# One projection bank between the quarters of row numbers, later weight loads behind the first gather, 38 warming transposes

## The chip, the cores and the metric

The kernel runs on one core of one Trainium2 chip. A core has five engines that run side by side, each with its own ordered instruction queue: TensorE (PE in the profile, with its weight loads listed as PEld), VectorE (DVE), ScalarE (ACT), GpSimd (POOL) and SyncE (SP), which here only issues transfers. Sixteen DMA engines move data between HBM and the on-chip memory. The metric is the device time of one execution in microseconds; the time before is the median of 3 runs.

## The reference

The input is `x`, 4096 tokens of 256 numbers, in float32. With `xn = layernorm(x)` the output is `x + attn(xn) + ffn(xn)`:

```python
# attn: local attention, 8 heads of 32, windows of 64 tokens, each query sees keys within 64
q, k, v = xn @ Wq + bq, xn @ Wk + bk, xn @ Wv + bv
p = softmax(where(abs(i - j) <= 64, q @ k.T * 32**-0.5, -1e30))
y = layernorm(xn + (p @ v) @ Wo + bo) * gamma + beta
attn = y + gelu(y @ W1 + b1) @ W2 + b2               # 256 -> 1024 -> 256
# ffn: mixture of 8 experts, the best 2 for each token
s = softmax(xn @ gate_w.T + gate_b);  top_w, top_idx = top_k(s, 2);  top_w /= top_w.sum()
ffn = sum over the 2 chosen e of top_w * (silu((xn @ gp_w[e].T + gp_b[e]) * (xn @ up_w[e].T + up_b[e]))
                                          @ down_w[e].T + down_b[e])   # 256 -> 816 -> 256
```

## The kernel before

All engines run in an order written out by hand (`manual_schedule`): each engine executes its instructions in the order in which the program issues them, and waits only on semaphores for its operands or for a buffer to come free.

**First part (lines 348 to 801).** Eight groups of 512 tokens are loaded (`load`), normalised (`stats`, `normal`: one group's rows are split over VectorE, ScalarE and POOL in group 0, later mostly POOL), stored to the DRAM table `xnd`, and transposed on TensorE (`turn`, L473). While the first load is in flight TensorE runs `WARM` transposes of the identity (L547), which write a bank that nobody reads. Router logits are taken from the transposed tokens (`logits`). Between these steps TensorE works off a list of 26 projection banks (`work`, handed out by `deal`): queries, keys and values of the first groups, each 512 columns wide, evacuated by ScalarE.

Then VectorE finds each token's two experts and, by prefix sums over counts, the place (`slot`) of each token in a table sorted by expert. The inverse table, which token stands in each row of the sorted table, is computed on TensorE. For each of four quarters of the 2 x 4096 slots VectorE builds two one-hot arrays, `in_row` (L753) and `in_col` (L758, then multiplied by the token number, L762), in two buffers each, and TensorE adds 16 products of them into the PSUM bank `found` (L764). After each of the first three quarters one projection bank is dealt (L771 and L772); the remaining three of the list are issued behind the last quarter (L782). `token` (L780) is `found` as integers.

Between the quarters VectorE also computes, in the pieces of `experts()`, which expert each unit uses (`expert`, L745). At the end of that piece SP loads unit 0's gate and up weights, unit 0's down weights and unit 1's gate and up weights (L746). The address of such a load is a value that SP reads from the `expert` table in on-chip memory (`value_load`, L207 and L215).

**Middle part (from line 1240).** The sorted table is worked off in units of 256 rows (or 128). For each, POOL gathers the unit's rows from `xnd` by indirect DMA, one per 128 rows (`gather`, L819), TensorE transposes them (`turned`, L832), ScalarE copies the first unit's transposes from PSUM (L837), and `chunk` runs the six 128-wide slices of the gated layer (L845), `down` the second product (L896, L907). Before the loop two gathers are issued (L1240), the remainder rows of `hT` are cleared (L1244), and the first residual tile is loaded on SP's queue and gets `bo` added on POOL (`residual`, L1066 and L1067).

Each of the first 32 steps of the loop also does one attention step for two tiles of 128 queries and four heads: scores on TensorE (L960), masked with their row minimum taken on VectorE (L974), exponentials on ScalarE (L989), the halves of each window merged on POOL (`merge`, L1001 and L1002), scaling on VectorE (`scale`, L1021), transposition on TensorE (`flip`, L1030). In step 0 TensorE's order is: scores, unit 0's transposes, chunks 0 and 1, unit 1's transposes, chunks 2 and 3, the flip, chunk 4. POOL's order in step 0 is: the residual's addition, unit 2's gather, the two subtractions of `apart` (L1009), then the merges. SP's order is: the three weight loads of L746, the residual, unit 1's down weights.

The last part runs the units that exist only for some routings (`whole`) and the second layer of the attention block (`hidden`, `second`); nothing in it is touched.

Of the kernel before, what the change touches and what calls it, by code (L numbers as in the profile page):

```python
# [34 lines left out]
I32 = mybir.dt.int32  # L35
# [6 lines left out]
P = 128  # L42
# [44 lines left out]
BLOCKS = len(UNITS)  # L87
# [4 lines left out]
DN = FCE * D + D  # L92
HQ = 4
AHEAD = 4
WARM = 50
EPS = 1e-5
MASKED = -1e30
LOWEST = -3e38
# [3 lines left out]
def block_kernel(ctx: ExitStack, tc: tile.TileContext, a: dict, out: bass.AP):  # L102
    nc = tc.nc
# [4 lines left out]
    def pool(stack, name, side=left, bufs=1, **kw):  # L108
        return stack.enter_context(
            tc.tile_pool(name=name, bufs=bufs, side=side, reuse_waits="tile", **kw)  # L110
        )

    const = pool(ctx, "const")
# [13 lines left out]
    def bank(name):  # L127
        return psm.tile([P, G], F32, tag="bank", name=name)
# [28 lines left out]
    slot = const.tile([P, 2, NT], I32, tag="slot", name="slot")  # L157
    share = const.tile([P, 2, NT], F32, tag="share", name="share")
    expert = const.tile([P, BLOCKS], I32, tag="expert", name="expert")
    token = const.tile([P, TILES], I32, tag="token", name="token")  # L160
    used = const.tile([P, len(MAYBE)], I32, tag="used", name="used")
    mv2 = const.tile([P, NT, 2], F32, tag="mv2", name="mv2")

    def bcast(ap, n, at):

        shape = list(ap.shape)
        shape.insert(at, n)
        return ap.unsqueeze(at).to_broadcast(shape)
# [29 lines left out]

    def expert_of(b):
        column = UNITS[b][2]  # L200
        return expert[0:1, column : column + 1]


    other = {}

    def load_gu(b):
        e = nc.sync.value_load(expert_of(b), min_val=0, max_val=E - 1)  # L207
        w = other.get(b, wexp).tile([P, GU], F32, tag="wg", name=f"wg{b}")
        nc.sync.dma_start(
            out=w, in_=a["gate_up"][bass.ds(e, 1), :, :].rearrange("e p n -> p (e n)")  # L210
        )
        return w

    def load_down(b):
        e = nc.sync.value_load(expert_of(b), min_val=0, max_val=E - 1)  # L215
        w = other.get(b, wexp).tile([P, DN], F32, tag="wd", name=f"wd{b}")
        nc.sync.dma_start(out=w, in_=a["down"][bass.ds(e, 1), :, :].rearrange("e p n -> p (e n)"))
        return w
# [129 lines left out]
    with ExitStack() as early:  # L348
# [64 lines left out]
        with ExitStack() as ln:  # L413
            xin = pool(ln, "xin", bufs=4)
            mvs, xs, xns, roots, scales = {}, {}, {}, {}, {}
# [112 lines left out]
            def deal(n):  # L528
                for _ in range(n):
                    list(next(todo))  # L530
# [14 lines left out]
            idle = bank("idle")  # L545
            for n in range(WARM):
                nc.tensor.transpose(idle[:, n % TG * P : (n % TG + 1) * P], ident, ident)  # L547
            copies = []
            for g in range(NG + 3):
# [37 lines left out]
                if 2 < g <= NG + 1 or g == 1:  # L587
                    n = max(g - 2, 0)
# [125 lines left out]
        def ended(name, numbers, n, ends_at):  # L714
            t = route.tile([P, n, E - 1], F32, tag=name, name=name)
            nc.vector.tensor_tensor(
                t, bcast(numbers, E - 1, 2), bcast(ends_at, n, 1), ALU.is_ge
            )
            return t

        def experts():

            expert_f = route.tile([P, BLOCKS], F32, tag="expert_f", name="expert_f")
            of_odd = route.tile([P, SINGLES], F32, tag="of_odd", name="of_odd")
            paired = route.tile([P, SINGLES], F32, tag="paired", name="paired")
            pe = ended("pair_e", pair_no[:, 0:BLOCKS], BLOCKS, pairs_to[:, 0 : E - 1])
            oe = ended("odd_e", single_no, SINGLES, odds[:, 1:E])
            nc.vector.tensor_tensor(
                paired,
                pair_no[:, PAIRS:BLOCKS],  # L730
                pairs_to[:, E - 1 :].to_broadcast([P, SINGLES]),
                ALU.is_lt,
            )
            yield
            single_e = expert_f[:, PAIRS:]
            nc.vector.tensor_reduce(expert_f, pe, AX.X, ALU.add)
            nc.vector.tensor_reduce(of_odd, oe, AX.X, ALU.add)
            yield
            nc.vector.tensor_tensor(single_e, single_e, of_odd, ALU.subtract)
            yield  # L740
            nc.vector.tensor_tensor(single_e, single_e, paired, ALU.mult)
            yield
            nc.vector.tensor_tensor(single_e, single_e, of_odd, ALU.add)
            yield
            nc.vector.tensor_copy(expert, expert_f)  # L745
            gus[0], downs[0], gus[1] = load_gu(0), load_down(0), load_gu(1)  # L746

        gus, downs = {}, {}
        table = experts()
        for n in range(4):  # L750
            k, q = n // 2, slice(n % 2 * QT, (n % 2 + 1) * QT)
            in_row = onehot.tile([P, P, QT], F16, tag="in_row", name=f"in_row{n}")
            nc.vector.tensor_tensor(  # L753
                in_row, row_of, bcast(part_f[:, 0, k, q], P, 1), ALU.is_equal
            )
            next(table, None)
            in_col = onehot.tile([P, TILES, QT], F16, tag="in_col", name=f"in_col{n}")
            nc.vector.tensor_tensor(  # L758
                in_col, col_of, bcast(part_f[:, 1, k, q], TILES, 1), ALU.is_equal
            )  # L760
            next(table, None)
            nc.vector.tensor_tensor(in_col, in_col, bcast(number[:, q], TILES, 1), ALU.mult)  # L762
            for i in range(QT):
                nc.tensor.matmul(  # L764
                    found[:, 0:TILES],
                    in_row[:, :, i],
                    in_col[:, :, i],
                    start=(n == 0 and i == 0),
                    stop=(n == 3 and i == QT - 1),
                )  # L770
            if n < 3:  # L771
                deal(1)  # L772

        z = col("z")
# [32 lines left out]
    def own(b, tag, shape, **kw):  # L807

        where = he
        if b >= ALWAYS:  # L810
            where, tag, kw = late, f"{tag}{b}", {}
        return where.tile(shape, F32, tag=tag, name=f"{tag}_{b}", **kw)

    def gather(b):
        x = own(b, "xs", [P, UNITS[b][1] if b >= ALWAYS else TB, D], bufs=3)
        at, n, _ = UNITS[b]
        for t in range(n):
            i = at + t
            nc.gpsimd.indirect_dma_start(  # L819
                out=x[:, t, :],  # L820
                out_offset=None,
                in_=xnd,
                in_offset=bass.IndirectOffsetOnAxis(ap=token[:, i : i + 1], axis=0),
            )
        return x
# [411 lines left out]
    def store(g, t, n, acc):  # L1237
        nc.sync.dma_start(out=rows(out, g * TG + t, n), in_=acc[:, t : t + n, :])

    xs = {b: gather(b) for b in range(2)}  # L1240

    hTs = [he.tile([P, FCE, B], F32, tag=f"hT{k}", name=f"hT{k}", bufs=1) for k in range(2)]
    for k in range(2):
# [15 lines left out]
    for b in range(ALWAYS):  # L1259
# [103 lines left out]
        n = b - (ALWAYS - len(MAYBE))  # L1363
# [22 lines left out]
    for b in range(ALWAYS, BLOCKS):  # L1386
        at, n, _ = UNITS[b]
# [139 lines left out]
```

## Time and profile before

| what | us |
|---|---|
| median of 3 runs (1086.47 to 1089.2) | 1088.48 |
| the profiled execution, its own time | 1084.23 |
| its span, first to last instruction | 1082.1 |
| PE busy | 1068.8 (99%) |
| PEld busy | 857.1 (79%) |
| DVE busy | 657.5 (61%) |
| ACT busy | 526.7 (49%) |
| POOL busy | 451.6 (42%) |
| PE busy in the first 40 us, in 40 to 80, in 80 to 120 | 37.79, 39.59, 36.51 |
| DMA share in the same stretches | 0.75, 0.34, 0.35 |

A timeline line of the profile gives the start in us from the span's beginning, the busy time in us, the engine, the line of the kernel with operation, result and operands, how many instructions are merged, and in brackets how long the engine was idle before and what ended that idle time. A line of waits gives the engine and the waiting work, what it waited for, and then the sum in us, the number of times and the longest. A busy PE is not PE at its peak: matmuls are pipelined, and their ends are modelled.

### The profile page before, as it was taken

What the parts mean: (1) busy time and instruction counts of PE and PEld (TensorE: products, weight loads), DVE (VectorE), ACT (ScalarE), POOL (GpSimd) and SP (SyncE); (2) the same over time, 40 slices, a digit from 0 to 9 for tenths busy, and PEclk for the clock granted to TensorE, in tenths of its full rate; (3) what the DMA queues carried; (4) which work ended last, traced back from release to release, by engine and by line L of the source; (5) the groups of instructions that cost most, each with busy time, mean ns of one, the idle gap of its engine ahead of it and who ended that gap; (6) DMA issues with size and microseconds to landing.
All of it is one profiled execution on the core that took longest, in us unless ns stands there. A gap on an engine that the chain in (4) does not pass through costs nothing. (4 is left out here: it accounts for less than half of the span.)

```text
span 1082.1 us, 19049 instructions
## 1 busy us (share of the span) xinstructions
PE 1068.8 (99%) x6802; PEld 857.1 (79%) x6802; DVE 657.5 (61%) x1709; ACT 526.7 (49%) x1225; POOL 451.6 (42%) x599
## 2 busy tenths in 40 slices
PE   9998999999999999999999999999999999999998
PEld 6577887887888788888888888888788847777778
DVE  6665766657666566666666766666533355555546
ACT  4526456654556546746564566455424363333320
POOL 5516544455445444554455535544520043322220
PEclk9999999999999999999999999999999999999999
DMA  8252445544445354545444545445666443333121
GB/s 282 76 215 97 142 140 179 178 144 154 159 143 192 125 174 149 201 142 175 159 175 142 197 142 189 142 161 169 191 213 228 158 146 105 101 98 97 59 64 40
DMA packets 61040, 163.42 MB, mean 151 GB/s; under 512 B 6576, under 2 KB 46896, under 8 KB 51472
## 3 DMA queue, kind: packets, MB, share of 16 engines
q1 hardware_dynamic: 53632, 144.18, 38.2%
q0 software_dynamic: 6480, 17.70, 6.1%
q8 instruction: 55, 0.90, 0.3%
q10 hardware_dynamic: 832, 0.30, 0.1%
q14 instruction: 41, 0.34, 0.1%
HBM read 140.28 MB, written 21.89 MB: 150 GB/s over the span
## 5 line engine op out<-in xcount | busy, mean ns | idle before, releaser
L845 PE MATMUL gu<-xsT,wg 128*128 128x256 f32 (+1 forms) x1632 | 363.1, 369 | 1.6 <-issue 1.5
L845 PEld LDWEIGHTS gu<-xsT,wg 128*128 128x128 f32 x1632 | 289.0, 190 | 46.9 <-DVE nm L974 8.6
L853 ACT ACTIVATE gs<-gu,wg 128x256 f32<-128x256 f32 (+1 forms) x204 | 92.4, 453 | 257.8 <-PE gu L845 254.8
L854 DVE SCALAR_TENSOR_TENSOR hT<-gu,wg,gs 128x256 f32<-128x256 f32 (+1 forms) x204 | 95.0, 467 | 177.0 <-ACT gs L853 173.6
L1001 POOL TENSOR_TENSOR pr<-pr 128x256 f32<-128x256 f32 x128 | 93.0, 727 | 247.9 <-ACT pr L989 247.9
L907 PE MATMUL pe<-wd,hT 128*128 128x256 f32 x768 | 171.6, 379 | 0.0
L907 PEld LDWEIGHTS pe<-wd,hT 128*128 128x128 f32 x768 | 145.4, 190 | 20.5 <-issue 1.0
L1172 POOL DMA_INDIRECT got<-done,slot x64 | 64.5, 1008 | 176.6 <-DVE acc L1185 109.4
L1002 POOL TENSOR_TENSOR pr<-pr,ident 128x256 f32<-128x256 f32 x128 | 125.2, 978 | 10.0
L989 ACT ACTIVATE pr<-pr,nm 128x256 f32<-128x256 f32 x256 | 126.8, 497 | 0.4
L1127 PE MATMUL ph<-x2T,W 128*128 128x512 f32 x256 | 111.4, 593 | 1.1 <-ACT x2T L1117 1.1
L974 DVE CUSTOM_DVE_ANT_0 pr<-ps,mask 128x256 f32<-128x256 f32 x256 | 90.7, 420 | 19.3 <-PE ps L960 19.3
L1134 ACT ACTIVATE hf<-ph,b 128x512 f32<-128x512 f32 x64 | 43.4, 688 | 116.5 <-PE ph L1127 57.9
L886 ACT ACTIVATE hT<-hT 128x512 f32<-128x512 f32 (+3 forms) x148 | 80.9, 546 | 32.0 <-DVE hT L854 21.8
L1127 PEld LDWEIGHTS ph<-x2T,W 128*128 128x128 f32 x256 | 48.0, 190 | 58.9 <-issue 52.9
L819 POOL DMA_INDIRECT xs<-xnd,token x71 | 68.8, 969 | 49.2 <-DVE paired_tiles L786 31.9
L1021 DVE TENSOR_TENSOR pr<-pr,rec 128x1024 f32<-128x1024 f32 x32 | 39.5, 1236 | 27.8 <-POOL pr L1001 27.8
L1208 DVE TENSOR_TENSOR acc<-u,acc 128x256 f32<-128x256 f32 x32 | 12.9, 423 | 70.9 <-ACT u L1211 70.3
L989 ACT ACT_TABLE_LOAD x31 | 39.8, 1283 | 23.8 <-DVE nm L974 23.7
L1022 DVE TENSOR_REDUCE same<-pr 128x8 f32<-128x1024 f32 x32 | 39.1, 1221 | 19.2 <-POOL pr L1002 19.2
L989 ACT ACTIVATION_READ_ACCUMULATOR pr<-pr,nm 128x1 f32 x256 | 48.5, 189 | 0.0
L1198 PE MATMUL s<-V,hv 128*128 128x128 f32 x384 | 44.2, 275 | 0.0
(231 smaller groups left out, 1572.0 us busy)
## 6 DMA issues: line engine op xcount, KB each, us to landing
wg<-in_gate_up SPq DMA_DIRECT2D x37, 1670.5 KB, 7.0
wd<-in_down SPq DMA_DIRECT2D x37, 1024.0 KB
done<-y SPq DMA_DIRECT2D x30, 256.0 KB
x<-in_x SPq DMA_DIRECT2D x8, 512.0 KB, 5.9
xnd<-xn SPq DMA_DIRECT2D x8, 512.0 KB
res<-xnd SPq DMA_DIRECT2D x16, 256.0 KB
x1d<-res SPq DMA_DIRECT2D x16, 256.0 KB
x<-x1d SPq DMA_DIRECT2D x8, 512.0 KB
```

The lines of the kernel that those rows point to most:

```text
L819: nc.gpsimd.indirect_dma_start(out=x[:, t, :], out_offset=None, in_=xnd, in_offset=bass.IndirectOffsetOnAxis(ap=token[:, i : i + 1], axis=0),)
L845: nc.tensor.matmul(pb[:, k, :], w[:, lo : lo + P], xT[:, c, :], start=(c == 0), stop=(c == DC - 1),)
L853: nc.scalar.activation(gs, pb[:, 0, :], AF.Identity, bias=w[:, gb : gb + 1])
L854: nc.vector.scalar_tensor_tensor(hT[:, f, :], pb[:, 1, :], w[:, ub : ub + 1], gs, ALU.add, ALU.mult)
L886: nc.scalar.activation(hT[on, lo:hi, :], hT[on, lo:hi, :], AF.Silu)
L907: nc.tensor.matmul(pd, hT[:, f, t * P : (t + 1) * P], w[:, f * D : (f + 1) * D], start=False, stop=(f == FCM - 1),)
L974: nc.vector.tensor_tensor_reduce(out=pr[:, hh, j, :], in0=ps[hh][:, j, :], in1=mask[:, kind + j, :], scale=-1.0, scalar=-LOWEST, op0=ALU.a ...
L989: nc.scalar.activation(pr[:, hh, j, :], pr[:, hh, j, :], AF.Exp, bias=nm[:, j, hh : hh + 1], scale=-1.0, accum_out=sums[:, j, hh : hh + 1],)
L1001: nc.gpsimd.tensor_tensor(first, first, second, ALU.add)
L1002: nc.gpsimd.tensor_tensor(second, second, bcast(ident, 2, 1), ALU.mult)
L1127: nc.tensor.matmul(ph, W1[:, c, f * P : (f + 1) * P], x2T[:, c, :], start=(c == 0), stop=(c == DC - 1),)
L1172: nc.gpsimd.indirect_dma_start(out=y, out_offset=None, in_=done, in_offset=bass.IndirectOffsetOnAxis(ap=slot[:, k, i : i + 1], axis=0),)
```

## The change

It has three parts. The number of warming transposes becomes 38 in place of 50. Of the projection banks dealt between the quarters, only the one after the second quarter stays; the other two are issued after the fourth quarter with the rest of the list, in unchanged order. And of the weight loads made when `expert` is ready, only unit 0's gate and up weights stay there. The other two are issued after unit 0's gather; they (and unit 1's down weights later) read their expert number from a copy of the table, `expert_then`, which POOL writes between unit 0's gather and unit 1's. No computation is added or left out otherwise.

```diff
-WARM = 50
+WARM = 38
@@ tables
     expert = const.tile([P, BLOCKS], I32, tag="expert", name="expert")
+    expert_then = const.tile([P, BLOCKS], I32, tag="expert_then", name="expert_then")
@@ def expert_of(b)
         column = UNITS[b][2]
-        return expert[0:1, column : column + 1]
+        table = expert_then if b < 2 and gus else expert
+        return table[0:1, column : column + 1]
+
+    gus, downs = {}, {}
@@ def experts()
             nc.vector.tensor_copy(expert, expert_f)
-            gus[0], downs[0], gus[1] = load_gu(0), load_down(0), load_gu(1)
-
-        gus, downs = {}, {}
+            gus[0] = load_gu(0)
+
@@ the loop over the four quarters
-            if n < 3:
+            if n == 1:
                 deal(1)
@@ ahead of the loop over the units
-    xs = {b: gather(b) for b in range(2)}
+    xs = {0: gather(0)}
+
+    nc.gpsimd.tensor_copy(expert_then, expert)
+    downs[0], gus[1] = load_down(0), load_gu(1)
+    xs[1] = gather(1)
```

## The prediction

> **What bounds the kernel now.** I read the page first: TensorE (PE) is busy 99% of the 1082.1 us span at a granted clock of 1.00, so only what moves PE's own sequence moves the end. The diff touches the first 100 us alone, so the next view is the list of waits in that stretch, then the timelines of PE, SP and POOL there. The waits:
>
> ```profile
> PE pts L832 <- DMA xs<-xnd,token: 2.3, 2, 1.2
> ...
> POOL res L1067 <- DMA res<-xnd: 1.1, 1, 1.1
> ```
>
> The first is the only wait of PE on a transfer: the transposes of unit 0 wait for the gathered rows. The second is POOL waiting for the second residual tile (at 133 us); the first one, at 80 us, is not waited for today. PE's timeline from the last quarter of `found` on (start, duration, engine, line, work, idle before):
>
> ```profile
> 71.99 2.34 PE L764 MATMUL found<-in_col,in_row 128*128 128x71 f16 x16
> 74.15 1.91 PE L296 MATMUL v<-Wv,xnT 128*128 128x256 f32 x8
> ...
> 79.42 1.15 PE L960 MATMUL ps<-kt,qt 32*128 32x256 f32 x16
> 81.71 0.30 PE L832 MATMUL pts<-ident,xs 128*128 128x128 f32 x1 [1.14 <-DMA xs<-xnd,token]
> 83.21 0.55 PE L832 MATMUL pts<-ident,xs 128*128 128x128 f32 x3 [1.20 <-DMA xs<-xnd,token]
> 84.44 3.72 PE L845 MATMUL gu<-xsT,wg 128*128 128x256 f32 x16 [0.68 <-issue]
> ...
> 92.53 0.65 PE L1030 MATMUL pT<-ident,pr 128*128 128x128 f32 x4 [0.48 <-DVE pr L1021]
> ```
>
> PE is idle 3.0 us in 80.6 to 84.4, of which 0.7 is the copy of the transposes. At 92.53 it waits for the scaled attention weights (L1021), a second chain that runs close behind. SP's DMA issues, and POOL:
>
> ```profile
> 65.70 0.37 SPq L209 DMA_DIRECT2D wg<-in_gate_up  x1
> 66.85 0.36 SPq L217 DMA_DIRECT2D wd<-in_down  x1
> 68.00 0.33 SPq L209 DMA_DIRECT2D wg<-in_gate_up  x1
> 68.44 0.38 SPq L1066 DMA_DIRECT2D res<-xnd  x1
> ```
>
> ```profile
> 74.89 1.17 POOL L819 DMA_INDIRECT xs<-xnd,token  x1 [31.88 <-DVE paired_tiles L786]
> ...
> 80.34 1.27 POOL L1067 TENSOR_TENSOR res<-res,bo 128x512 f32<-128x512 f32 x1
> ...
> 90.49 0.73 POOL L1001 TENSOR_TENSOR pr<-pr 128x256 f32<-128x256 f32 x1
> ```
>
> The reader is to see that the residual tile `res` is fourth in SP's queue, issued 12 us before POOL adds `bo` to it, and that POOL's add stands ahead of the merges (L1001) on which L1021 waits.
>
> **The change, part by part** (times on today's axis; the gain at the start is put in at the end).
>
> *The quarters.* Today each quarter takes 2.16 us of PE and each bank 1.74 (60.28, 62.43, 64.17, 66.34, ... are their starts), and PE never waits. Afterwards quarter 2 follows quarter 1 at 62.43, but its `in_col` is ready only at 62.51 (VectorE's L762: 61.76 + 0.75), and PE's first matmul about 0.2 later: 0.3 us of new PE idle. Quarter 2 then ends at 64.9, the q bank at 66.6, quarter 3 at 68.8. VectorE's fourth `in_row`, which waits 1.17 us for quarter 2 today, starts at 65.4 and its `in_col` is done 2.67 later at 68.1, so quarter 4 runs 68.8 to 70.95 without a wait. `token` then comes 3.2 us earlier, and the first gather starts at 71.7 instead of 74.89. The two banks only change sides, so PE reaches `ps` at 79.42 + 0.3 = 79.7.
>
> *Unit 0's gather.* Today the gather of each tile lands 5.65 and 5.9 us after POOL is done issuing it (76.06 to 81.71, 77.31 to 83.21), while the DMA share is 1.0. Afterwards only `wg0` is ahead of it (6.8 us from issue to landing: 72.5). A gather on idle DMA engines issued by 96.35 has moved its bytes by 98.0, so about 2 us; the second is issued by 74.1 and lands before 77, well under `ps`. PE goes on without waiting: `ps` ends at 80.9, four transposes 0.66 (the row at 87.99 less overlap), copy 0.6, so `gu` starts at 82.2 instead of 84.44: a gain of 2.2 us there. Four chunks and unit 1's transposes take 7.6 (84.44 to 92.05), so PE wants the flip at 89.8.
>
> *What moves behind the gather.* `expert_then` costs POOL a copy of 39 numbers (0.22 us by L409's 128x40 cast), done by 74.35. SP's value load now waits for it, and behind that load stand all its later issues: `wd0`, `wg1`, `res`, `wd1`. Today SP issues 0.99 us after `expert` is written (64.71 to 65.70), and then at 1.15, 1.15 and 0.44 us steps. So `wd0` goes at 75.34, `wg1` 76.5, `res` 76.9 (8.5 us later than today), `wd1` 78.1. The weights are hidden: by the arithmetic below `wd0` lands near 80.6 (PE needs it at 100.3), `wg1` near 84.6 (needed at 100.9). Unit 1's gather now meets them; at today's 5.9 us it lands at 83.0, needed at 86.
>
> `res` is not hidden. A `wg` alone takes 6.6 to 6.8 us from issue to landing: 1.71 MB at the saturated 428 GB/s is 4.0, leaving 2.8 fixed (the lone `res` at 130.15 is released 2.9 later: 0.6 for its 0.26 MB and 2.3). `wg0` takes 6.8 although four transfers were queued behind it, so I take the queue to be served in order. Then `res` lands after `wd0` 1.05 + `wg1` 1.71 + itself 0.26 = 3.02 MB: 7.1 + 2.8 = 9.9 us from 75.34, that is 85.2, and up to 0.6 later if unit 1's gather (0.26 MB) shares the engines; with 2.3 for the fixed part 84.7. Bounds 84.7 to 85.8; I take 85.4. The same sum today gives 65.70 + 4.73/0.428 + 2.8 = 79.6, just under the 80.34 at which POOL wants it, which agrees with no wait.
>
> POOL is free for L1067 at 77.7 and now stands until 85.4. From its start to the end of the `xd` pair is 4.54 us today (80.34 to 84.88: the add, two gathers for unit 2, two subtractions); then four L1001 and three L1002 without ScalarE's pauses, at 1.49 a pair: 5.2. The last L1001 ends at 95.15; L1021 takes 1.22 (91.25 to 92.47), and the flip starts at 96.45 instead of 92.53: **+3.9 us**. PE, ready at 89.8, idles 6.65 us; VectorE, in order, stands too, and everything after the flip hangs on the same chain as today (PE waits 0.3 for L1034 at 98.22 already), so nothing is won back.
>
> *The clock.* No PE idle of today's trace past the start is longer than 1.2 us. How a cold PE runs can be seen only in the warming transposes, 20 weight loads early and 20 late:
>
> ```profile
> L547 PEld LDWEIGHTS idle<-ident x20: 231/231/231, 1.9 to 5.9; 128*128 128x128 f32 x20
> ```
>
> ```profile
> L547 PEld LDWEIGHTS idle<-ident x20: 139/140/142, 7.4 to 9.4; 128*128 128x128 f32 x20
> ```
>
> They come at 0.21 us, then at 0.105: half pace for the first 5.4 us (1.58 to about 7), although the clock row shows 1.00 throughout. [...] No row here shows a fall. By the trace alone the new idle costs itself; [...] **+2.5 us**; ends 0 and 2.7.
>
> *38 warming transposes.* The 12 removed are warm ones: 12 x 0.105 = 1.3 us, so they end at 8.4 instead of 9.65. The first `xn` is done by 8.6 to 9.04, so the transposes end some 0.9 earlier. But group 1's transposes then wait for POOL's `xn` (done 15.51, used 15.75), whose VectorE chain gains only the 0.25 us by which ScalarE's root comes sooner. Ends 0.2 and 0.9, by those two limits; nearest to the tighter one: **-0.4**.
>
> *Sum.* +3.9 + 2.5 - 0.4 = +6.0 us. On the profiled execution, 1084.2 (span 1082.1 and 2.1 around): 1090.2. The median of the runs, 1088.5, lies 4.3 above that execution, so the median I predict is **1094.5**.
>
> **The rivals.**
> 1. *The wait without the clock* (17%): PE stays warm through the idle. +3.5: 1092.0. For it: no row shows a fall. Against: the start of this trace runs at half pace for 5.4 us.
> 2. *`res` is hidden; not slower* (12%): the small transfer is served beside the large ones and lands about 2.9 us after its issue, at 79.8. POOL's chain then ends at 89.55 and the flip starts at 90.9: -1.7 - 0.4 = -2.1, so 1086.4. Against: `wg0`'s landing, undisturbed by what followed. It decides from a landing before 81.9, where the flip is no later than today net of the start.
> 3. *Something else is late too* (5%): the gather meeting `wd0` late, or the shorter warming leaving PE cold for the first projections; +8 or more, 1096.5 and up.
> That the gather isn't sooner at all is excluded by PE's order: quarter 4 loses two banks ahead of it, and VectorE is ready.
>
> **How the numbers follow.** The likeliest case (66%) is wait and clock: 1092.5 (`res` at 84.7, clock 1.7, start 0.9) to 1095.3 (85.8, 2.7, 0.2) by its bounds, and the runs shown scatter by about 1.3 around their middle. Rival 1's lowest, by the same ends, is 1090.8. With the scatter on both sides the range is 1089.0 to 1097.0; it leaves out most of rivals 2 and 3. A difference under 0.3% (3.3 us) can't be told from none in this kernel. Slower by more than that: nearly all of the likeliest (0.63), half of rival 1 (0.09), rival 3 (0.04): 0.76. Within: the rest of those (0.11) and most of rival 2 (0.09): 0.20. Faster: 0.04.
>
> **What would show it.** Gather 0 about 3.5 us earlier and no wait of PE on `xs`; POOL's L1067 released by the `res` transfer after some 7.5 us of idle; PE idle over 6 us before the first L1030, and matmuls after it at twice today's spacing. If L1067 starts near 80, the prediction is wrong; if it starts at 85 and PE is not slow afterwards, the clock term is.

## The result, and the profile after

The changed kernel takes 1093.02 us in the median of six runs (1091.75 to 1093.88), the kernel before 1086.67 in the median of six (1086.44 to 1089.2): 1.0051 times as long, interval 1.0039 to 1.0063. It is slower, by 6.35 us between the medians. Its profiled execution took 1091.75 us (span 1090.0) where that of before took 1084.23 (span 1082.1): +7.5.

First the waits of its first 160 us (engine and waiting work, what it waited for, sum, times, longest):

```profile
POOL res L1069 <- DMA res<-xnd: 10.8, 2, 9.8
...
PE pT L1032 <- DVE pr L1023: 5.7, 1, 5.7
```

PE's wait on `xs` is gone from the list. In its place POOL waits 9.8 us for the first residual tile, and PE 5.7 us for the scaled attention weights. SP's and POOL's timelines show where the tile stands in the queue:

```profile
65.02 0.37 SPq L212 DMA_DIRECT2D wg<-in_gate_up  x1
74.30 0.36 SPq L220 DMA_DIRECT2D wd<-in_down  x1
75.44 0.33 SPq L212 DMA_DIRECT2D wg<-in_gate_up  x1
75.87 0.54 SPq L1068 DMA_DIRECT2D res<-xnd  x1
```

```profile
70.87 1.17 POOL L821 DMA_INDIRECT xs<-xnd,token  x1 [28.36 <-DVE paired_tiles L788]
...
86.31 1.28 POOL L1069 TENSOR_TENSOR res<-res,bo 128x512 f32<-128x512 f32 x1 [9.81 <-DMA res<-xnd]
...
95.25 0.72 POOL L1003 TENSOR_TENSOR pr<-pr 128x256 f32<-128x256 f32 x1
```

The gather starts 4.02 us sooner than before (70.87 against 74.89), but the residual is issued 7.4 us later (75.87 against 68.44) and its addition starts 5.97 us later (86.31 against 80.34). The last merge follows it by the same distance (+4.76). PE's timeline from the last two quarters on:

```profile
65.79 4.52 PE L766 MATMUL found<-in_col,in_row 128*128 128x71 f16 x32
70.13 3.67 PE L243 MATMUL q<-xnT,Wq 128*128 128x512 f32 x4
73.60 4.57 PE L299 MATMUL v<-Wv,xnT 128*128 128x256 f32 x16
...
81.53 1.15 PE L962 MATMUL ps<-kt,qt 32*128 32x256 f32 x16
83.94 3.72 PE L847 MATMUL gu<-xsT,wg 128*128 128x256 f32 x16 [0.68 <-ACT xsT L839]
...
97.29 1.11 PE L1032 MATMUL pT<-ident,pr 128*128 128x128 f32 x4 [5.74 <-DVE pr L1023]
98.19 3.62 PE L847 MATMUL gu<-xsT,wg 128*128 128x256 f32 x8
...
108.27 3.72 PE L847 MATMUL gu<-xsT,wg 128*128 128x256 f32 x16
```

Two things are to be read from the durations. Behind the flip, 8 `gu` products take 3.62 us, as long as 16 of them take when nothing is wrong (3.72 at 83.94): half pace. And the first q bank behind the quarters takes 3.67 us, where a bank took 1.91 before (the row at 74.15 in the kernel before): half pace as well, at a place where PE waits for nothing. The windows of the same execution, cut to the microsecond near where the clock changes (stretch, its length, busy time and instructions of PE, PEld, DVE, ACT and POOL, granted clock, DMA share, GB/s):

```profile
66.00:69.00 3.00, 3.00 (x24) 3.00 (x23) 2.86 (x6) 0.69 (x1) 0.00 (x0) 0.95 1.02 339
69.00:76.00 7.00, 7.00 (x21) 4.50 (x20) 2.56 (x11) 0.69 (x1) 4.34 (x6) 0.53 0.47 154
76.00:96.00 20.00, 14.88 (x75) 10.61 (x73) 4.02 (x19) 11.28 (x29) 9.46 (x14) 1.00 0.61 224
96.00:103.00 7.00, 5.71 (x19) 4.89 (x20) 5.77 (x10) 0.47 (x1) 3.38 (x3) 0.51 0.07 19
```

The clock falls twice, each time for 6.83 us, twice 3.413 (68.69 to 75.52 and 96.00 to 102.83 in the trace's record of the clock). That record begins at 7.25, and the four times stand 18, 20, 26 and 28 times 3.413 us behind its beginning; the windows of 3.41 us that are spoken of below are counted in that way. The second fall is the one that was predicted, after the idle stretch. The first, at 69 to 76, was not: PE is shown as busy all the time ahead of it.

So the time goes as follows. The flip starts 4.76 us later (97.29 against 92.53). Unit 1's first chunk started at 100.94 in the kernel before:

```profile
100.94 3.72 PE L845 MATMUL gu<-xsT,wg 128*128 128x256 f32 x16
```

From the flip to it, it is 10.98 us instead of 8.41 (97.29 to 108.27, against 92.53 to 100.94): +2.57. That makes 7.33 at unit 1; the last product of the kernel comes 7.58 later than before, and 0.3 more arises in the closing transfers: +7.9 us of span. The 2.65 us that the first fall costs the five banks behind the quarters (70.13 to 81.53 is 11.40 us, where 5 x 1.75 = 8.75) are not in this sum: PE was done with everything ahead of the flip at 91.55 and waited for POOL.

### The profile page after: what moved, and what is told of

The parts are those of the page before. It is cut to its first block, busy times and chain, and to the rows that moved or that the text cites. A ratio compares the mean times of both kernels' runs of the same rounds, so it can differ in the third digit from the quotient of the medians.

```text
span 1090.0 us, 19027 instructions
## 1 busy us (share of the span) xinstructions
PE 1073.3 (98%) x6790; PEld 859.5 (79%) x6790; DVE 657.2 (60%) x1709; ACT 527.0 (48%) x1225; POOL 451.5 (41%) x600
## 5 line engine op out<-in xcount | busy, mean ns | idle before, releaser
L1032 PE MATMUL pT<-ident,pr 128*128 128x128 f32 x256 | 39.4, 277 | 5.7 <-DVE pr L1023 5.7
```

## The experiments

The theory was that one late transfer, the first residual, stops POOL; that POOL's in-order queue makes the flip late; and that PE's idle stretch then halves its clock. The rivals were that the wait costs only itself (no clock term), that the three parts are each harmful, and, once the first fall had been seen, that the two adjacent fp16 quarters are what is harmful. All kernels compute the whole reference. "Before" is the median of the kernel before on the same chip; chips differ by up to 1.8 us, so ratios are compared, not medians. The last three kernels of the table ran on a chip on which the kernel before takes 1084.90, some 1.5 us less than on the others; their expectations, given in us, are to be read with that difference.

| kernel | median us | before | ratio, interval | granted clock |
|---|---|---|---|---|
| e1_res_ahead | 1083.81 | 1086.08 | 0.9980, 0.9971 to 0.9989 | 0.995 to 0.998 |
| e2_three_banks | 1095.81 | 1086.08 | 1.0089, 1.0075 to 1.0102 | 0.992 to 0.995 |
| e3_filled_idle | 1091.01 | 1086.08 | 1.0045, 1.0032 to 1.0059 | 0.994 to 0.997 |
| e4_res_ahead_three_banks | 1084.00 | 1086.08 | 0.9976, 0.9966 to 0.9986 | 0.998 to 1.000 |
| e5_warm_only | 1085.64 | 1086.41 | 0.9997, 0.9989 to 1.0006 | 0.996 to 1.000 |
| e6_banks_only | 1085.93 | 1086.41 | 1.0000, 0.9991 to 1.0008 | 0.994 to 0.998 |
| e7_loads_only | 1095.90 | 1086.41 | 1.0098, 1.0083 to 1.0114 | 0.994 to 0.995 |
| e8_gathers_ahead | 1083.50 | 1086.41 | 0.9979, 0.9970 to 0.9988 | 0.996 to 1.000 |
| e9_held_clock | 1081.84 | 1084.90 | 0.9976, 0.9967 to 0.9984 | 0.999 to 1.000 |
| e11_add_behind | 1082.16 | 1084.90 | 0.9980, 0.9972 to 0.9989 | 0.993 to 0.998 |
| e10_add_and_gather_behind | 1079.26 | 1084.90 | 0.9954, 0.9940 to 0.9967 | 0.999 to 1.000 |

### e1_res_ahead: the residual's load ahead of the deferred weights

From the changed kernel; the load alone is moved, POOL's addition stays where it was.

```diff
-    def residual(i):
+    def residual_load(i):
 ...
         nc.sync.dma_start(out=res, in_=rows(xnd, i, 2))
+        return res
+
+    def residual(i, res=None):
+        res = residual_load(i) if res is None else res
         nc.gpsimd.tensor_tensor(res, res, bcast(bo, 2, 1), ALU.add)
 ...
+    first_res = residual_load(0)
     nc.gpsimd.tensor_copy(expert_then, expert)
 ...
-    res = {0: residual(0)}
+    res = {0: residual(0, first_res)}
```

> The changed kernel, with only the first residual's load issued ahead of the deferred weight loads; its addition on POOL stays where it is. Theory (the residual behind 2.8 MB of weights stops POOL, and PE's idle then halves its clock): POOL's addition starts near 76.5 us without a wait, the flip near 92 instead of 97.3, no fall of the clock after it; about 7.5 us less than the changed kernel, 1085.5 us, with the clock's fall at 68.8 to 75.5 us still there. Rival (the deferred weights themselves cost, by colliding with unit 1's gather or by coming late): the time stays near 1093.

Measured: 1083.81, that is 0.9980 of before, where the change stood at 1.0051, and 1.7 us less than expected (some 0.6 of that is the chip, on which the kernel before takes 1086.08 instead of 1086.67). POOL's and PE's timelines of this kernel:

```profile
78.22 1.27 POOL L1074 TENSOR_TENSOR res<-res,bo 128x512 f32<-128x512 f32 x1
```

```profile
64.27 3.45 PE L243 MATMUL q<-xnT,Wq 128*128 128x512 f32 x4
...
92.28 0.66 PE L1032 MATMUL pT<-ident,pr 128*128 128x128 f32 x4 [0.47 <-DVE pr L1023]
```

The addition no longer waits, the flip is back at 92.28 with the 0.47 us of idle that it had before, and no half pace follows it. One transfer of 0.26 MB in the wrong place in SP's queue is the whole loss, 0.7% of the kernel. What remains is the fall in the quarters: the q bank between them takes 3.45 us.

### e11_add_behind: everything stays late, POOL just doesn't stand

From the changed kernel. All transfers are issued in the order of the changed kernel, so the residual lands as late as there; only POOL's addition is moved behind the merges of step 0, on which the flip hangs.

```diff
-    res = {0: residual(0)}
+    first_res, res = residual_load(0), {}
 ...
             merge(pr, 3)
+            if b == 0:
+                res[0] = residual(0, first_res)
```

> The changed kernel, its transfers all as they are and the residual landing near 86.5 us as before, but with POOL's addition to it moved behind the four merges of step 0. Theory (what costs is that POOL's queue stands behind the addition, not that the residual is late): the flip near 92, no fall after it, as in the first experiment, 1083.8. Rival (the late transfers themselves cost): over 1088.

Measured: 1082.16, ratio 0.9980, as with the load moved. POOL's timeline:

```profile
90.30 0.73 POOL L1003 TENSOR_TENSOR pr<-pr 128x256 f32<-128x256 f32 x1
...
92.84 1.27 POOL L1074 TENSOR_TENSOR res<-res,bo 128x512 f32<-128x512 f32 x1
```

SP issues the residual at 77.17 here and it lands 11.3 us later, near 88.5, later even than in the changed kernel (86.3), and the flip starts at 92.34 all the same. So the late transfer costs nothing by itself. What cost was urgent work standing behind a patient instruction in an in-order queue.

### e3_filled_idle: the wait stays, the idle is filled

From the changed kernel: 48 transposes of the identity into a bank that is overwritten later, in front of the first flip. They end well ahead of the flip, so the wait is unchanged and only PE's idleness goes.

```diff
             if b == 0:
+                for n in range(48):
+                    nc.tensor.transpose(pos[i][:, n % 2, n // 2 % DC, :], ident, ident)
                 prT0 = flip(i, hq, 0, pr)
```

> The changed kernel, with 48 transposes of the identity on PE in the idle before the first flip, written to a bank that is overwritten later. Theory (PE's idle halves its clock for two windows after the flip): the flip stays near 97.3 us, the clock stays at 1.00 there, and the time is 2.6 us less than the changed kernel, 1090.4. Rival (the clock falls for another reason, or transposes don't hold it): 1093, with the clock at 0.50 at 96 to 103 us.

Measured: 1091.01, ratio 1.0045: 4.9 us above before. The changed kernel was not run on this chip; its own ratio is 1.0051, so the medians differ by about 0.7 us, and the two intervals overlap. The 2.6 us that were expected do not show in the time. The clock does show the difference in every run: 0.994 to 0.997 in the five runs here, 0.992 or 0.993 in the six of the changed kernel. And the profile says where the time went: in this execution the first fall of the clock hits the bank between the quarters, and everything from the gather on happens 1.8 us later (`wd0` is issued at 76.13 instead of 74.30), which takes back most of what is won. Windows and PE's timeline:

```profile
96.00:100.00 4.00, 2.07 (x18) 1.78 (x17) 1.59 (x2) 0.00 (x0) 3.44 (x4) 1.00 0.00 0
100.00:104.00 4.00, 4.00 (x22) 3.44 (x21) 3.96 (x9) 1.78 (x4) 2.49 (x4) 1.00 0.09 19
```

```profile
91.74 5.40 PE L1364 MATMUL po<-ident 128*128 128x128 f32 x48
99.07 0.66 PE L1032 MATMUL pT<-ident,pr 128*128 128x128 f32 x4 [1.93 <-DVE pr L1023]
...
107.49 3.72 PE L847 MATMUL gu<-xsT,wg 128*128 128x256 f32 x16
```

The clock stays at 1.00 through the flip and after it, the four transposes of the flip take 0.66 us instead of 1.11, and from the flip to unit 1's first chunk it is 8.42 us (99.07 to 107.49), the value of before (8.41), not the changed kernel's 10.98. So the term of 2.57 us is the clock, and it is PE's idleness that brings it. That no clock term exists (rival 1 of the prediction) is excluded.

The run also shows that transposes can keep the clock up: 5.4 us of nothing but fp32 transposes held it here (granted 1.00 from 88 to 104 us), and the warming transposes of every kernel here reach full pace by themselves (one every 0.21 us, then one every 0.105).

### e2_three_banks and e7_loads_only: the deferred loads without the bank moves

The first is the changed kernel with all three banks between the quarters again; the second also has 50 warming transposes, so it is the kernel before with the weight loads deferred and nothing else.

```diff
-            if n == 1:
+            if n < 3:
                 deal(1)
```

```diff
-WARM = 38
+WARM = 50
```

(The second kernel has both edits.)

> The changed kernel, with the three projection banks back between the quarters. Theory (the residual's landing sets the flip): no fall of the clock at 69 us, PE reaches the scores 2.6 us sooner, but the gather, the loads behind it and so the flip come 3.3 us later, near 100.6; about 3.3 us more than the changed kernel, 1096.3. Rival (the clock's fall during the quarters is a main part of the loss): 2.6 us less, 1090.4.

> The kernel before, with the deferred loads alone (50 warming transposes, three banks). Theory (the residual's landing sets the flip and the idle halves the clock): the flip near 102 us, PE idle 10 us before it, 9.5 us over the kernel before. Rival (the loss belongs to the banks): within 2 us of it.

Measured: 1095.81 (1.0089) and 1095.90 (1.0098), slower than the whole change. PE's timelines, of the first and of the second:

```profile
101.53 1.11 PE L1032 MATMUL pT<-ident,pr 128*128 128x128 f32 x4 [10.17 <-DVE pr L1023]
```

```profile
102.51 1.11 PE L1032 MATMUL pT<-ident,pr 128*128 128x128 f32 x4 [7.70 <-DVE pr L1023]
```

With the banks back between the quarters the gather, and with it `wd0`, comes about 3.6 us later (77.89 against 74.30 in the first), the addition at 90.58 instead of 86.31, and the flip with it (101.53 instead of 97.29). So the deferred loads are the loss, and moving the banks softens it: it brings the gather, and so everything queued behind the gather, forward. A second wait appears in both, 2.1 to 2.5 us on unit 1's gather, which now meets `wd0` and `wg1`.

### e5_warm_only and e6_banks_only: the other two parts alone

Both from the kernel before: `WARM = 38`, and `if n == 1:` ahead of `deal(1)`.

> The kernel before, with 38 warming transposes in place of 50 alone. Theory: PE starts 0.7 us sooner and keeps it up to the quarters; 0.5 us under the kernel before. Rival (the shorter warming costs clock at the start): not under it, with the clock below 1.00 in the first 20 us.

> The kernel before, with one bank between the quarters in place of three alone. Theory (two quarters of small fp16 products in a row let the clock fall, whichever way the loads go): clock at 0.50 for some windows between 60 and 78 us in nearly every run, PE reaches the scores near 82 us; the gather comes 3 us sooner and is no longer waited for, which about balances it: within 1 us of the kernel before. Rival (the fall at 69 us came from something else in the changed kernel): no fall, 2.2 us under the kernel before.

Measured: 1085.64 and 1085.93 against 1086.41, ratios 0.9997 and 1.0000, both intervals across 1. Neither part alone can be told from no change. The profiles say a little more. The quarters start at 59.59 to 60.23 in the profiled executions of all kernels with 38 transposes and at 60.28 to 61.42 in those with 50, which agrees with the small gain predicted for the start, in single executions only. And with the banks alone two new losses stand against the gather that comes 0.8 us sooner (74.09 against 74.89) and is no longer waited for. PE's and POOL's timelines of e6:

```profile
65.89 3.33 PE L240 MATMUL q<-xnT,Wq 128*128 128x512 f32 x4
...
73.35 3.46 PE L240 MATMUL q<-xnT,Wq 128*128 128x512 f32 x4
```

```profile
83.40 1.27 POOL L1067 TENSOR_TENSOR res<-res,bo 128x512 f32<-128x512 f32 x1 [3.79 <-DMA res<-xnd]
```

Both banks behind a pair of quarters run at half pace, and POOL waits 3.79 us for the residual even with the loads in their old order: it lands 16.5 us after `wg0` is issued (66.86), where the sum of the prediction, 4.73 MB / 0.428 + 2.8, gives 13.9. Unit 0's gather is issued 7.2 us after `wg0` here, 9.2 us after it before: the trace shows 100 of its packets and of unit 1's ahead of the residual's last one, where before there was none.

### e9_held_clock: filler between the adjacent quarters

From e1 (so without POOL's wait): 12 transposes of the identity into an unused bank behind quarters 1 and 3.

```diff
+            if n % 2 == 0:
+                if n == 0:
+                    hold = bank("hold")
+                for m in range(12):
+                    nc.tensor.transpose(hold[:, m % TG * P : (m % TG + 1) * P], ident, ident)
             if n == 1:
                 deal(1)
```

> The changed kernel with the residual's load ahead (as in the first experiment), and 12 transposes of the identity after the first and after the third quarter. Theory (two quarters of small fp16 products in a row count as too little work and let the clock fall): no stretch at 0.50 between 60 and 78 us; each dozen costs 1.3 us, so the time is about that of the first experiment, 1083.5 to 1084.5. Rival (the clock falls there for a reason that has nothing to do with what PE runs): still at 0.50 for some 3.4 us or more, and 2 us over the first experiment.

Measured: 1081.84, ratio 0.9976, and all 13 runs within 0.5 us of each other (1081.69 to 1082.2), where e1's 11 runs span 3.4. The granted clock is 0.999 or 1.000 in each run, where e1 never came above 0.998. PE's timeline and the windows:

```profile
61.86 1.49 PE L777 MATMUL hold<-ident 128*128 128x128 f32 x12
```

```profile
68.00:72.00 4.00, 4.00 (x34) 4.00 (x33) 2.05 (x5) 0.00 (x0) 0.00 (x0) 1.00 0.89 368
72.00:76.00 4.00, 4.00 (x18) 2.87 (x17) 2.36 (x10) 0.69 (x1) 2.18 (x3) 1.00 0.12 35
```

No fall is left, where e1 has a granted clock of 0.50 from 64 to 66 us and from 72 to 74. The time is under the expected 1083.5 to 1084.5, also when 1.2 us for the chip are taken off. So it is what PE does between the quarters that decides about the clock. As a gain the filler is about even: its 24 transposes cost 2.6 us and save what the falls cost, `ps` starts at 81.48 against 81.78 in e1, and the two ratios' intervals overlap. Real work between the quarters, as the three banks are, holds the clock for nothing (granted 1.00 from 64 to 76 us in the kernel before).

### e4_res_ahead_three_banks and e8_gathers_ahead: what comes up next

e4 has the edits of e1 and e2 together. e8 adds to them that both first gathers are issued ahead of the deferred loads:

```diff
-    xs = {0: gather(0)}
+    xs = {b: gather(b) for b in range(2)}

+    first_res = residual_load(0)
     nc.gpsimd.tensor_copy(expert_then, expert)
     downs[0], gus[1] = load_down(0), load_gu(1)
-    xs[1] = gather(1)
```

> The changed kernel with both edits: residual's load ahead, and three banks between the quarters. Theory: no fall of the clock anywhere and no wait for the residual; unit 0's gather is issued near 74.2 on idle DMA engines and lands before the scores are done, so the chunks start near 81.5 and the flip near 91, bound by POOL's merges; 1.5 us under the kernel before, 1085.2. Rival (deferring the weights costs by itself): over the kernel before.

> The changed kernel with three banks, the residual's load ahead, and both first gathers ahead of the deferred weights. Theory (unit 1's gather meets the weights in the run with the first two edits, costing 2.4 us of wait and a fall of the clock): PE waits for neither gather, the flip comes near 91.1 us, no fall after 60 us; 1082.5 us. Rival (the weights now come too late, for unit 0's down product or unit 1's chunks near 99 us): PE waits there, over 1084.

Measured: 1084.00 (0.9976) and 1083.50 (0.9979). The first is under the time that was expected, but by another way: PE does wait for a gather, and the clock does fall. The second is a miss by 1 us. PE's timelines, of e4 and of e8:

```profile
87.73 0.55 PE L834 MATMUL pts<-ident,xs 128*128 128x128 f32 x3 [2.45 <-DMA xs<-xnd,token]
88.12 5.31 PE L847 MATMUL gu<-xsT,wg 128*128 128x256 f32 x16
```

```profile
91.13 1.01 PE L1032 MATMUL pT<-ident,pr 128*128 128x128 f32 x4 [2.11 <-DVE pr L1023]
```

In e4 the wait has moved to unit 1's gather, which meets the deferred weights; in e8 that wait is gone, and PE waits 2.11 us for POOL, whose addition and third gather (3.7 us, 80.09 to 83.80) stand ahead of the merges. In both profiled executions a fall of the clock follows the idle stretch, short as it is (granted clock 0.57 in 88 to 92 us of e4, 0.66 in 92 to 96 of e8): in e4 the 16 products behind it take 5.31 us instead of 3.62. Not every run has it: of e4's nine, five have a granted clock of 0.998 like the profiled one, four 0.999 or 1.000. PE waits for no weights in e8, so the rival of late weights falls. Of e8's twelve runs six have a granted clock of 0.999 or more and a median of 1082.6, six a lower one and 1084.4.

### e10_add_and_gather_behind: both lessons together

From e8: the residual's addition and the third gather are issued behind `scale` of step 0, so POOL goes to the merges first.

```diff
-    res = {0: residual(0, first_res)}
+    res = {}
 ...
-        if b + 2 < ALWAYS:
+        if 0 < b < ALWAYS - 2:
             xs[b + 2] = gather(b + 2)
 ...
             scale(i, hq, pr, sums, xd)
+            if b == 0:
+                res[0] = residual(0, first_res)
+                xs[2] = gather(2)
```

> The changed kernel with three banks, both first gathers and the residual's load ahead of the deferred weights, and POOL's addition and unit 2's gather behind step 0's last use of POOL. Theory (in the run with both gathers ahead POOL's chain sets the flip, and PE's 2.1 us of idle before it still lets the clock fall in some runs): the flip near 89.6, PE idle under 1 us, clock at 1.00 in nearly all runs; 1081.5. Rival (something behind the flip waits for unit 2's gather or the addition): 1083.5 or over.

Measured: 1079.26 (1079.13 to 1079.33), ratio 0.9954, interval 0.9940 to 0.9967: faster than both kernels of the case, and, with the chip's 1.5 us allowed for, about 0.7 us faster than expected. PE's timeline:

```profile
89.51 0.66 PE L1032 MATMUL pT<-ident,pr 128*128 128x128 f32 x4 [0.48 <-DVE pr L1023]
```

The flip starts 3.0 us sooner than before (92.53), and no run has a clock below 0.999, where the 25 runs of before on this chip have 0.997 to 0.999. Of the 5.6 us between the medians the flip explains 3.0; the rest fits what one fall of the clock costs (1.7 to 2.65 us in these traces), and that part was not measured by itself.

## Why the prediction was right, step by step

**The quarters: right in what it said, and one thing not seen.** Quarter 2's new idle was 0.14 us in the profile (4.46 us for the first pair, where two quarters take 4.32), 0.3 predicted; no wait of quarter 4 appeared; the gather came 4.0 us sooner, of which 0.69 is the earlier start and 3.3 the banks (3.2 predicted). But "PE reaches `ps` at 79.42 + 0.3 = 79.7" failed: `ps` starts at 81.53, because the clock fell to half in the quarters. The step took the banks as movable at a constant price; e9 shows that fp32 work in their place holds the clock (granted 1.00 from 64 to 76 us, where the changed kernel has 0.59 in 68 to 72 and 0.56 in 72 to 76). The failure stayed without consequence for the time only because PE had to wait for POOL anyway. In e1, e6 and e11 it is on the path.

**Unit 0's gather: right in effect.** PE does not wait for it. The gain that was written at `gu`, 2.2 us, was 0.5 (83.94 against 84.44), by the same fall.

**The residual: right in mechanism, short in size.** The addition was to start at 85.4, less 0.4 for the start; it started at 86.31. `wd0` was issued 0.6 us sooner than I had it, and the residual landed 12.0 us after that issue instead of the 10.06 of my sum. The trace has every DMA packet, and the size tells whose it is (13,364 bytes for gate and up weights, 8,192 for down weights, 1,024 for the residual, 4,096 for a gather), so the 12.0 us can be taken apart, in busy time averaged over the 16 engines:

| part | predicted, us | in the trace, us |
|---|---|---|
| issue to the first packet, and last packet to POOL | 2.8 | 1.0 + 0.4 |
| `wd0`, `wg1` and the residual | 7.1 | 2.9 + 4.2 + 0.7 |
| unit 1's gather | 0.2, at most 0.6 | 1.5 |
| packets of `wd1` that ran before the residual's last one | none | 0.9 |

Some 0.3 us are left, idle time and the end of unit 0's gather. The mis-sized terms are the gather's share and the packets of `wd1`, of which the sum expected none ahead of the residual's last one. The gather's packets took 0.16 us in more than half of the cases, and up to 1.4 us among those of `wg1`. And the residual's own packets are spread over 2.4 us (83.47 to 85.87), where before it was 1.6 (77.66 to 79.28). The order was the one I had taken: the first of them starts when five sixths of `wg1` have been started. The same sum also came out short in e6 (13.9 against 16.5) and e7 (12.3 us from `wd0`'s issue to the addition), where 100 and 64 packets of gathers lie ahead of the residual's last one. In the kernel before none does; there that last packet ends at 79.28, and the sum, 79.6, holds. In the trace of the changed kernel the packets of unit 1's gather, 64 of 4,096 bytes, run among those of the two weight loads, not behind them; so my "up to 0.6 later" for the sharing was the place to be generous. Why a gather's packet takes so much longer among those of `wg1` is open.

**From the addition to the flip: right.** 10.98 us against 11.05. With the landing, the flip is 1.24 us later than predicted, net of the start (97.29 against 96.05).

**The clock: right, and the row that showed no fall was no evidence.** +2.57 against +2.5. That idle would bring a fall was shown by no trace of before, and the size was my estimate: half of the 5.4 us for which the warming transposes run at half pace there is 2.7, the upper end; the lower one, 1.7, had no trace behind it. e3 shows the cause. PE's idle was 5.74 us, not 6.65, since PE itself came late; it still filled a whole window of 3.41 us, 92.59 to 96.00 (PE busy 0.00 of 3.41 us), and the fall begins at 96.00. The trace of before showed no fall although PE stood for 3.0 us between 80.6 and 84.4; I had looked at single waits, of which none was over 1.2 us, but in these traces a fall goes with the idle time that lies in one window: 1.71 us at most there, and no fall; 2.23 in e5, and a fall (shown under the sum).

**The start: not decided.** -0.4 predicted, -0.69 in the one profiled execution; in the time of e5 nothing that can be told from zero.

**The sum: errors that partly cancelled, and that is luck.** The span moved by 7.9 us where I had 6.0: 1.2 from the flip, 0.1 from the clock, 0.55 behind them. The median moved by less, 6.35, and lies only 1.3 above the profiled execution where I had added 4.3. The failed step is "The median of the runs, 1088.5, lies 4.3 above that execution", carried over as a constant. Of the 3.0 us between, 1.8 is the small sample: the median of before is 1088.48 in the three runs that I had and 1086.67 in six. The other 1.2 fits a stall that the change removes. On the chip of e5, 7 of 32 runs of before have a granted clock of 1.000, as the profiled execution of before has, and a median of 1084.49; the other 25 have 0.996 to 0.998 and 1086.61. Where 2.1 us like these can go is seen in the profile of e5, which is the kernel before but for its warming. PE's timeline there:

```profile
84.18 5.41 PE L845 MATMUL gu<-xsT,wg 128*128 128x256 f32 x16 [0.68 <-ACT xsT L837]
```

The `gu` products lose 1.7 us to a fall of the clock. Both kernels stall here for unit 0's gather and the copy behind it, some 3 us in all. In both, the stretches below are windows of 3.41 us counted from the first record of the clock in the trace, first for the kernel before, then for e5:

```profile
78.77:82.18 3.41, 2.10 (x19) 0.87 (x17) 1.59 (x9) 0.94 (x2) 3.15 (x5) 1.00 1.00 397
82.18:85.59 3.41, 1.70 (x8) 1.36 (x9) 1.25 (x8) 1.79 (x6) 2.54 (x5) 1.00 0.38 117
```

```profile
81.10:84.51 3.41, 1.18 (x6) 0.76 (x7) 2.28 (x14) 0.97 (x3) 2.94 (x5) 1.00 0.60 212
84.51:87.93 3.42, 3.42 (x10) 2.70 (x9) 0.00 (x0) 1.32 (x7) 1.89 (x4) 0.50 0.16 43
```

In the kernel before, the border of two windows parts the stall, 1.31 us and 1.71, and the clock stays. In e5 2.23 us of it lie in one window, and the clock is at half for the next. The changed kernel does not wait for this gather; so its runs save there what the profiled execution of before never lost. No profile was taken of a run of the kernel before with a lower clock, so this is shown for e5 and inferred for it.

**Rivals.** 1 (wait without clock) falls by the clock of 0.51 behind the flip and by e3. 2 (the residual is hidden) falls by the 9.81 us at L1069. Of 3 (something else is late too) the gather meeting `wd0` exists, but only with three banks between the quarters (e2, e4, e7), and a cold first projection does not: in the changed kernel the k projections start 0.84 us sooner.

## What to carry to other kernels

When loads are moved on a queue, list every later transfer of that queue and put the small one with a near consumer ahead of the large ones; then look at the consumer's own engine, and move whatever can be patient behind whatever sets the end. Of these two cures each alone brought back the whole loss (e1, e11), and both together, with the three banks in their old place and both first gathers ahead of the deferred loads, beat the kernel before by 0.46% (e10). Before a stage like the fp16 quarters is pushed together, or a stall of 2 us or more accepted, price the clock that may fall behind it (1.7 to 2.65 us a fall here), and take the distance between a profiled execution and the median apart before carrying it over.

## What the runs showed of the hardware

- In each of the 13 profiled executions the record of the clock begins at the point from which the warming transposes come at twice their pace (4.7 to 7.4 us after the start; 7.09 in the kernel before, 7.25 in the changed one), and every later change stands a whole number of 3.41 us behind it. Of the windows of 3.41 us counted in that way 16 were followed by a fall, leaving out the end, where PE has no work left: in 7 of them PE was idle for 2.11 us or more (2.11 in e8, 3.41 in the changed kernel), in 9 it ran fp16 quarters (128 x 71 products) for 2.74 us or more (2.90 in the changed kernel). None of the other windows at full clock, some 4,000, was; they have at most 1.71 us of idle time (the kernel before) and at most 2.37 us of the quarters. What happens in between was not met.
- So a PE that the profile shows as busy without a gap can still lose its clock: two quarters in a row last 4.3 to 4.5 us, and the window ahead of the changed kernel's first fall, 65.28 to 68.69, has PE busy for all of its 3.41 us. No fall came where a quarter of 2.2 us and an fp32 bank of 1.74 stood in turn (granted 1.00 from 64 to 76 us in the kernel before, e4, e8 and e10), nor where 1.3 us of fp32 transposes stood between the quarters (e9, 1.00 in the same stretch). Why the fp16 products go with a fall and the fp32 ones do not is not shown.
- The fp16 quarters themselves did not get longer: the second pair of the changed kernel takes 4.34 us with the clock falling inside it, the first 4.46 at full clock. The price was paid by the fp32 banks behind them (rows of 3.0 to 3.7 us instead of 1.9).
- A fall lasted one window (12 of the 16), two (3) or, where PE stood for 10.17 us, four (e2: 93.53 to 107.19). It ended with the first window that held no idle time and at most 1.33 us of the quarters. One fall cost 1.7 us (e5) to 2.65 (the first of the changed kernel). The windows lie elsewhere in each execution (their count begins 4.7 to 7.4 us after the start), and stalls of some 3 us in all brought no fall in the profiled execution of the kernel before and one in e5's. That this makes most of the scatter of e8 (medians of 1082.6 and 1084.4 by the granted clock) and of the kernel before (1084.49 and 1086.61) is my estimate.
- In the first 7 us of the kernel before, the granted-clock row shows 1.00 while the warming transposes run at half pace. The trace has no record of the clock ahead of 7.1 us, so that 1.00 is no proof of full pace.
